# Layernorm of a feed-forward on turned tokens, beside a local attention on one NeuronCore

## The chip, the cores and the metric

The kernel runs on one NeuronCore of a Trainium2 chip. TensorE (PE) multiplies matrices and turns them, VectorE (DVE), ScalarE (ACT) and GpSimd (POOL) work on tiles, and SyncE (SP) issues the DMAs. The metric is the device time of one execution in microseconds. All data is float32.

## The reference, cut to what matters

A decoder layer on `x` of 8 x 256 x 128: a state-space block, a cross-attention, and then six layers of local attention and feed-forward. The change is in the feed-forward of those six layers:

```python
def shift_tokens(t):
    a, s = jnp.split(t, 2, -1)
    s = jnp.pad(s, ((0, 0), (1, 0), (0, 0)))[:, :-1]
    return jnp.concatenate([a, s], -1)

def ffn_layer(x, g, bln, W1, b1, W2, b2):
    mu = x.mean(-1, keepdims=True)
    var = ((x - mu) ** 2).mean(-1, keepdims=True)
    xn = (x - mu) / jnp.sqrt(var + 1e-05) * g + bln
    hg = xn @ W1 + b1
    a, gate = jnp.split(hg, 2, -1)
    return a * jax.nn.gelu(gate, approximate=False) @ W2 + b2

for i in range(DEPTH):
    x = attn_layer(shift_tokens(x), Wqkv[i], q_scale[i], k_scale[i], Wo[i]) + x
    x = ffn_layer(shift_tokens(x), ln_g[i], ln_b[i], W1[i], b1[i], W2[i], b2[i]) + x
```

Mean and variance go over the 128 features of a token.

## The kernel before, in words

Activations lie with the 128 features on the partitions and tokens along the free axis. A pair of batches is one tile of 128 x 512 (`x3[p]`), a batch is 256 columns of it.

Stages one and two (state space, cross-attention) end near 690 us. The third stage runs the list `seq` of 48 entries (six layers times eight batches) through a table written out by hand, `slots` (L1178). `run(n)` (L1212) goes once through its four rows for each batch and calls each named step for batch `n`, `n + 1`, `n + 2` or `n - 1`, so several batches are in flight. The steps that matter here:

- `query_key` (L881): two products into `qk_ps` (L875), two VectorE products with the rotation tables (L892, L893), two GpSimd adds (L896) and ScalarE's squares `sq` (L898). `squares` adds them up (L905), `root` takes the roots on ScalarE (`ss`, `rn`, through `inv_root`, L98), `normalise` multiplies on GpSimd (L924).
- `value` (L916): `v_ps` (L875) and its copy by ScalarE (L918).
- `turn` (L926): eight transposes into `qkT_ps` (L931) and a copy by ScalarE into `qT` (L938) or `kz` (L941).
- `scores` (L979), `masked` (L991), `peak` (L1000, and L1001 on GpSimd), `weigh` (exp of `pw` on ScalarE), `add_weights` (L1012, L1013, and L1014 on GpSimd).
- `turn_weights` (L1016): four transposes into `pT_ps` (L1021), copied by ScalarE (L1025). `attend` (L1038, L1046) and `project_out` (`y_ps`, L1052 and L1060) follow.
- `"ff"`, once a row, and `"late"`, in odd runs, take the next step of `feed_forward` (L1067), a generator that handles one pair during eight rows. There are 23 such pairs; the last pair of the last layer is taken in two halves.

In `feed_forward` before the change, `late` shifts tokens into `xs` (L1087 to L1089). Then, for each half `c` of the pair, TensorE multiplies `xs` with the full 128x128 matrix `mean_w` (all entries 1/128), which gives the mean of each token on every partition (`ln_mu`, L1101). VectorE subtracts (L1102), ScalarE squares (L1103). One product with `mean_w` over all 512 columns gives the variance (`ln_var`, L1106), ScalarE takes Ln and Exp, VectorE multiplies (L1108) and ScalarE adds the bias (L1109). The products of the feed-forward (`f_ps`, L1122) read the result `xn`.

PSUM tiles come from three groups: `big` (two buffers of two banks: `qk_ps`, `v_ps`, `qkT_ps`, `f_ps`), `s` (two buffers of one bank, banks 6 and 7: `ln_mu`, `ln_var`, `pT_ps`, `y_ps`, part of `f_ps`) and `two`. A new tile waits for the readers of the tile whose buffer it takes. TensorE and VectorE execute in the order in which the code calls them (`manual_schedule`, L1360). The order on ScalarE and GpSimd is chosen by the framework's scheduler when the program is built; each engine then works strictly in its order.

Of the kernel before, what the change touches and what calls it, by code (L numbers as in the profile page):

```python
# [9 lines left out]
FP = mybir.dt.float32  # L10
AF = mybir.ActivationFunctionType
ALU = mybir.AluOpType
AX = mybir.AxisListType

P = 128
B, S, D = 8, 256, 128
NPAIR = B // 2
TP = 2 * S
# [31 lines left out]
def decoder_kernel(ctx: ExitStack, tc: tile.TileContext, a: dict, out: bass.AP):  # L50
    nc = tc.nc
    V, A, G, T = nc.vector, nc.scalar, nc.gpsimd, nc.tensor
# [3 lines left out]
    lnp = ctx.enter_context(tc.tile_pool(name="lnp", bufs=2))  # L56
# [5 lines left out]
    def ps_big(name):  # L62
        return banks[-1].tile([P, 1024], FP, tag="big", name=name)

    def ps_s(name):
        return banks[-1].tile([P, 512], FP, tag="s", name=name)
# [10 lines left out]
    ident = keep.tile([P, P], FP, name="ident")  # L77
# [3 lines left out]
    mean_w = keep.tile([P, P], FP, name="mean_w")  # L81
    G.memset(mean_w, 1.0 / D)
    eps_t = keep.tile([P, 1], FP, name="eps_t")
# [5 lines left out]
    def col(name, i=0, n=P):  # L89
        o = _OFF[name] + i  # L90
        return cols[:n, o : o + 1]
# [3 lines left out]
    def with_table(f, *args, **kw):  # L95

        with tc.issue_after(table[-1].ins) if table else ExitStack():
            return f(*args, **kw)  # L98
# [3 lines left out]
    def load_table(name="natural_log_exp_and_others"):  # L102

        late = name == "exp_and_others" and logs
        with tc.issue_after(logs[-1].ins) if late else ExitStack():
            table.append(tc.keep_in_program_order(A.preload_act_table_set(name)))

    def inv_root(dst, src, bias=0.0):

        logs.append(with_table(A.activation, dst, src, AF.Ln, bias=bias))  # L110
        return with_table(A.activation, dst, dst, AF.Exp, scale=-0.5)
# [189 lines left out]
    with (  # L301
# [450 lines left out]
        for p in range(NPAIR):  # L752
            c = pairs[p]
# [313 lines left out]
    def feed_forward(d, p, b=None):  # L1067


        w1, w2 = wts[d][1:3]  # L1070
        at = slice(0, TP) if b is None else slice(b * S, (b + 1) * S)
        m = at.stop - at.start
        x = x3[p][:, at]
        if b == 0:

            t0, t1 = (pools3["w"].tile([P, INNER], FP, tag="wqkv", name="fw", bufs=4) for _ in range(2))
            xs, hh = t0[:, :m], t0[:, m : 4 * m]
            xn, gts = t1[:, :m], [t1[:, (1 + j) * m : (2 + j) * m] for j in range(3)]
        else:
            xs = pools3["b"].tile([P, TP], FP, name="fxs", bufs=1)[:, :m]  # L1080
            xn = pools3["b"].tile([P, TP], FP, name="fxn", bufs=1)[:, :m]
            hh, gts = None, []
        parts = [slice(i, i + S) for i in range(0, m, S)]

        def late(i):

            G.memset(xs[HD:, i : i + 1], 0.0)  # L1087
            A.copy(xs[:HD, i : i + S], x[:HD, i : i + S])
            A.copy(xs[HD:, i + 1 : i + S], x[HD:, i : i + S - 1])  # L1089

        for c in parts:
            late(c.start)
            if len(parts) > 1 and not c.start:
                yield
        if len(parts) == 1:
            yield
        xc = lnp.tile([P, TP], FP, name="ln_xc")[:, :m]
        sq = lnp.tile([P, TP], FP, name="ln_sq")[:, :m]
        for c in parts:
            mu = ps_s("ln_mu")[:, :S]  # L1100
            T.matmul(mu, lhsT=mean_w, rhs=xs[:, c], start=True, stop=True)  # L1101
            V.tensor_tensor(xc[:, c], xs[:, c], mu, ALU.subtract)  # L1102
            A.activation(sq[:, c], xc[:, c], AF.Square)  # L1103
            yield
        var = ps_s("ln_var")[:, :m]
        T.matmul(var, lhsT=mean_w, rhs=sq, start=True, stop=True)  # L1106
        inv_root(sq, var, eps_t)
        V.scalar_tensor_tensor(xn, xc, col("ff_g", d), sq, ALU.mult, ALU.mult)  # L1108
        A.activation(xn, xn, AF.Identity, bias=col("ff_b", d))  # L1109
        yield  # L1110
        if b != 0:
            hh = pools3["b"].tile([P, 3 * TP], FP, name="fh", bufs=1)[:, : 3 * m]
        hh = hh.rearrange("p (j t) -> p j t", j=3)

        def up(i, blocks):

            if blocks[0] < 2:
                pr = ps_big("f_ps")
            for j in blocks:
                f0, n = FB[j]  # L1120
                o = (pr[:, j * TP : j * TP + m] if j < 2 else ps_s("f_ps")[:, :m])[:n]
                T.matmul(  # L1122
                    o, lhsT=w1[:, i * DFF + f0 : i * DFF + f0 + n], rhs=xn, start=True, stop=True
                )
                yield j, n, o

        def product(j, n, o):
            V.scalar_tensor_tensor(
                hh[:n, j, :], o, col("ff_b1", d * 6 + j, n), gts[j][:n], ALU.add, ALU.mult
            )  # L1130

        gates = list(up(1, (0, 1, 2)))
        yield

        for j, n, o in gates:
            if b != 0:
                gts.append(pools3["b"].tile([P, TP], FP, name="fg", bufs=3)[:, :m])
            with tc.issue_after(turned[-1].ins), tc.issue_after(rooted[-1].ins):
                A.activation(gts[j][:n], o, AF.Gelu, bias=col("ff_b1", d * 6 + 3 + j, n))
        load_table()  # L1140
        if b != 0:
            yield
        for blocks in ((2,), (0, 1)):
            for block in list(up(0, blocks)):
                product(*block)
            yield
        for c in parts:
            y_ps = ps_s("f2_ps")[:, :S]
            for j, (f0, n) in enumerate(FB):
                T.matmul(y_ps, lhsT=w2[:n, j, :], rhs=hh[:n, j, c], start=(j == 0), stop=(j == 2))  # L1150
            V.scalar_tensor_tensor(x[:, c], y_ps, col("ff_b2", d), x[:, c], ALU.add, ALU.add)
            yield
# [48 lines left out]
    queue, turned, rooted, copied = [], [], [], []  # L1201
# [10 lines left out]
    def run(n):  # L1212
        nonlocal ff
        for f, *args in slots:
            k, *args = args or [0]
            if f == "ff" or (f == "late" and n % 2):
                next(ff, None)
            elif f == "late":
                pass
            elif f == "end":  # L1220
                if k != n % 2:
                    next(end)
            elif 0 <= n + k < len(seq) and (f, n + k, *args) not in done:
                f(n + k, *args)
                if f is project_out and args[0]:
                    d, b = seq[n + k]
                    last = d == DEPTH - 1
                    if b % 2:
                        ff = feed_forward(d, b // 2)
                        next(ff)  # L1230
                    elif last and b == B - 2:
                        queue.extend((feed_forward(d, b // 2, 0), finish(b // 2, 0)))
                    if last and b % 2 and b > 1:
                        queue.append(finish(b // 2 - 1))
# [27 lines left out]
    with tc.tile_pool(name="s2", bufs=2, reuse_waits="tile") as sp:  # L1262
# [52 lines left out]
        for p in range(NPAIR):  # L1315
# [17 lines left out]
            for hb in range(NHB):  # L1333
                T.matmul(
                    y_ps, lhsT=w2["wo"][:, hb, :], rhs=oT[:, hb, :], start=(hb == 0), stop=(hb == NHB - 1)
# [11 lines left out]
    with ExitStack() as st:  # L1347
# [12 lines left out]
        with tc.manual_schedule(engines={mybir.EngineType.PE, mybir.EngineType.DVE}):  # L1360
            shift(1)
            for n in range(-1, len(seq)):
                run(n)
            project_out(len(seq) - 1, 0)
            attend(len(seq) - 1, 1)
            for _ in ff:
                pass
            next(end)
            project_out(len(seq) - 1, 1)
            tail = feed_forward(DEPTH - 1, NPAIR - 1, 1)  # L1370
            queue.append(finish(NPAIR - 2))
            while queue:
                next(tail, None)
                next(end)
            for _ in tail:
                pass
            for _ in finish(NPAIR - 1, 1):
                pass
# [86 lines left out]
```

## Time and profile before

| what | value |
|---|---|
| median of 3 runs | 2244.76 us (2239.37 to 2244.81) |
| span of the profiled execution | 2235.6 us |
| median above that span | 9.2 us |
| TensorE clock granted, mean | 0.969 |
| TensorE busy | 2096.8 us (94%) |
| VectorE busy | 1743.8 us (78%) |
| GpSimd busy | 1636.2 us (73%) |
| ScalarE busy | 1422.2 us (64%) |

The page does not list a time of the profiled execution apart from its span, so the median stands for what lies around it. A span runs from the first to the last instruction. In the views below a row gives the start, the duration, the engine, the line and the tiles written and read; in brackets is how long the engine sat idle before and who released it. Matmuls on TensorE overlap, so how long it is occupied is read from one start to the next. "PEld" is the weight load of a matmul.

### The profile page before, as it was taken

How to read it: one execution, taken by the hardware profiler on the slowest of the kernel's cores; microseconds unless marked ns; L12 is line 12 of the kernel's file. 1: busy time of each engine (PE TensorE's matmuls, PEld its weight loads, DVE VectorE, ACT ScalarE, POOL GpSimd, SP SyncE). 2: the span in 40 equal slices, each digit the busy share in tenths (PEclk: the TensorE clock that was granted, in tenths of full speed). 3: DMA queues.
4: the chain of work that ended last, by engine and by line, in shares of the span. 5: the costliest groups of instructions: out<-in, count | busy, mean ns of one | idle time of the engine just before them, and what ended most of it. 6: DMA issues, size and time to landing. Idle time of an engine off the chain costs nothing.

```text
span 2235.6 us, 77068 instructions
## 1 busy us (share of the span) xinstructions
PE 2096.8 (94%) x32482; PEld 1314.8 (59%) x32482; DVE 1743.8 (78%) x2533; ACT 1422.2 (64%) x2432; POOL 1636.2 (73%) x1440
## 2 busy tenths in 40 slices
PE   7787879999998999999999999999999999999986
PEld 3232334444445766666767767676767767676663
DVE  5988986353467988888888888888888888888762
ACT  4544546455556776777767677777767677777554
POOL 3988985132268988888888888888888888888750
PEclk8888889999999999999999999999999999999998
DMA  4434431000204444334443434343443434333330
GB/s 124 119 104 100 105 102 31 1 5 1 83 7 68 71 71 95 67 71 75 74 88 71 79 65 94 68 79 67 75 88 69 78 67 84 68 65 64 65 62 10
DMA packets 438326, 155.41 MB, mean 70 GB/s; under 512 B 401886, under 2 KB 418140, under 8 KB 437852
## 3 DMA queue, kind: packets, MB, share of 16 engines
q1 hardware_dynamic: 437500, 150.10, 34.2%
q8 instruction: 255, 4.18, 0.8%
q14 instruction: 91, 0.75, 0.1%
q10 hardware_dynamic: 480, 0.38, 0.1%
HBM read 54.68 MB, written 1.31 MB: 25 GB/s over the span
## 4 chain that ended last, share of the span: by engine, by line
PE 73%; DVE 13%; ACT 7%; issue 4%; POOL 3%; DMA 0%; SPq 0%; DVEq 0%; POOLq 0%; ACTq 0%
PE qk_ps L875 13%; PE y_ps L1052 8%; PE qkT_ps L931 7%; PE o_ps L1038 7%; PE f_ps L1122 6%; PE v_ps L875 6%; PE s_ps L979 5%; DVE m L691 4%; PE pT_ps L1021 3%; PE f_ps L1150 3%; PE o_ps L1296 2%; PE pr L279 2%; PE s_ps L1277 2%; DVE wz L721 2%; ACT ln_sq L98 1%
## 5 line engine op out<-in xcount | busy, mean ns | idle before, releaser
L896 POOL TENSOR_TENSOR qk<-qk,rb 128x512 f32<-128x512 f32 x384 | 481.0, 1275 | 49.0 <-DVE rb L893 30.6
L924 POOL TENSOR_TENSOR qk<-qk,rn 128x1024 f32<-128x1024 f32 x192 | 365.5, 1904 | 12.8 <-ACT rn L98 12.8
L875 PE MATMUL qk_ps<-wqkv,xs 128*128 128x512 f32 x768 | 363.3, 595 | 2.4 <-ACT kz L941 1.4
L1001 POOL TENSOR_TENSOR pw<-pw,mx 128x512 f32<-128x512 f32 x192 | 202.1, 1052 | 164.6 <-DVE mx L1000 164.3
L898 ACT ACTIVATE sq<-qk_ps 128x1024 f32<-128x1024 f32 x192 | 197.0, 1026 | 165.8 <-PE o_ps L1038 122.6
L892 DVE TENSOR_TENSOR qk<-qk_ps,tab 128x1024 f32<-128x1024 f32 x192 | 228.9, 1192 | 66.6 <-PE qk_ps L875 65.1
L905 DVE TENSOR_REDUCE ss<-sq 128x16 f32<-128x1024 f32 x192 | 229.4, 1195 | 6.2 <-ACT sq L898 6.1
L893 DVE TENSOR_TENSOR rb<-qk_ps,tab 128x1024 f32<-128x1024 f32 x192 | 233.3, 1215 | 0.0
L1014 POOL TENSOR_TENSOR pw<-pw,mx 128x512 f32<-128x512 f32 x192 | 200.4, 1044 | 39.1 <-ACT fxn L1109 32.0
L1286 POOL TENSOR_TENSOR ws<-w 128x512 f32<-128x512 f32 x64 | 81.4, 1272 | 196.8 <-ACT w L98 154.1
L1052 PEld LDWEIGHTS y_ps<-oT,wo 128*128 128x128 f32 x1536 | 186.2, 192 | 46.6 <-issue 33.5
L931 PE MATMUL qkT_ps<-ident,qk 128*128 128x128 f32 x1536 | 210.6, 280 | 2.9 <-POOL qk L924 2.9
L1052 PE MATMUL y_ps<-oT,wo 128*128 128x128 f32 x1536 | 187.5, 275 | 1.9 <-ACT pT L1025 1.6
L1046 DVE STREAM_TRANSPOSE oT<-o_ps 128x512 f32<-128x512 f32 x192 | 126.1, 695 | 80.9 <-PE o_ps L1038 80.9
L875 PEld LDWEIGHTS qk_ps<-wqkv,xs 128*128 128x128 f32 x768 | 131.2, 191 | 97.2 <-issue 92.7
L979 PEld LDWEIGHTS s_ps<-kz,qT 64*32 64x32 f32 x12288 | 138.2, 105 | 74.5 <-issue 33.4
L875 PE MATMUL v_ps<-wqkv,xs 128*128 128x512 f32 x384 | 180.5, 592 | 0.3 <-ACT sq L898 0.3
L931 PEld LDWEIGHTS qkT_ps<-ident,qk 128*128 128x128 f32 x1536 | 165.9, 141 | 23.0 <-POOL qk L924 3.8
L98 ACT ACTIVATE ab<-dt,aa 128x512 f32<-128x512 f32 x128 | 87.6, 689 | 143.1 <-DVE m L691 142.9
L726 POOL TENSOR_TENSOR dw<-wz 128x512 f32<-128x512 f32 x128 | 133.9, 1046 | 56.1 <-DVE wz L721 56.1
L691 DVE TENSOR_TENSOR_SCAN m<-dw,ab 128x256 f32<-128x256 f32 x256 | 160.9, 669 | 12.8 <-POOL mc L693 11.4
L1038 PE MATMUL o_ps<-vz,pT 64*32 64x64 f32 x12288 | 168.0, 225 | 1.7 <-issue 1.7
(217 smaller groups left out, 4178.7 us busy)
## 6 DMA issues: line engine op xcount, KB each, us to landing
vz<-v SPq DMA_DIRECT2D x1152, 64.0 KB, 2.2
rows<-bc_dram SPq DMA_DIRECT2D x126, 256.0 KB, 3.9
vz<-v SPq DMA_DIRECT2D x576, 32.0 KB, 2.1
wqkv<-in_L_ffn_Wqkv SPq DMA_DIRECT2D x18, 512.0 KB, 4.4
wo<-in_L_ffn_Wo SPq DMA_DIRECT2D x48, 64.0 KB, 2.6
w<-in_L_ffn_W SPq DMA_DIRECT2D x6, 341.0 KB, 3.1
t_in<-in_x SPq DMA_DIRECT2D x4, 256.0 KB, 3.4
wkv<-in_L_xattn_Wkv SPq DMA_DIRECT2D x1, 1024.0 KB, 7.9
```

Of the source, the lines that this page charges most:

```text
L691: V.tensor_tensor_scan(m[:, t], i["dw"][:, t], i["ab"][:, t], 0.0, ALU.add, ALU.mult)
L875: T.matmul(pr[:, i * 512 : (i + 1) * 512], lhsT=got[n]["xs"][:, tb * P : (tb + 1) * P], rhs=thirds[seq[n][0], c][:, i * 512 : (i + 1) * 51 ...
L892: V.tensor_tensor(t, p3, cs, ALU.mult)
L893: V.tensor_tensor(rb, p3, sn, ALU.mult)
L896: G.tensor_tensor(t[:, :, o], t[:, :, o], rb[:, :, f], ALU.add)
L905: V.tensor_reduce(got[n]["ss"][:, 2 * c + tb, :], got[n]["sq"], AX.X, ALU.add)
L924: G.tensor_tensor(t, t, r, ALU.mult)
L931: T.transpose(t_ps[:, hb * P : (hb + 1) * P], t[:, 2 * hb : 2 * hb + 2, :].rearrange("p h d -> p (h d)"), ident,)
L979: T.matmul(s_ps[i * W : (i + 1) * W, e, c : c + 2 * W], lhsT=qT[r, 4 * g + i, j * W : (j + 1) * W], rhs=kz[r, 4 * g + i, k0 : k0 + 2 * W], ...
L1001: G.tensor_tensor(pw, pw, mx[:, 0].unsqueeze(3).to_broadcast([P, 4, 2, 2 * W]), ALU.subtract)
L1038: T.matmul(o_ps[i * W : (i + 1) * W, e, c : c + HD], lhsT=pT[r, j, i * W : (i + 1) * W], rhs=vz[r, j, i, :], start=True, stop=True, tile_p ...
L1052: T.matmul(y_ps[:, :P], lhsT=wts[d][0][:, hb, :], rhs=got[n]["oT", wh][:, hb // 4, (hb // 2) % 2, :].rearrange("p (w h q) -> p h w q", w=4 ...
```

## The change

The layernorm of the feed-forward is done with tokens on the partitions. For each half, TensorE turns two blocks of 128 tokens into PSUM (`ft_ps`); VectorE takes mean and variance of each token with `bn_stats` and `bn_aggr` and negates the mean; ScalarE takes the root of the variance (a column of numbers now, not a full tile); GpSimd multiplies the negated mean with it; ScalarE normalises each block out of PSUM with these as scale and bias. One step later TensorE turns the two blocks back (`fn_ps`), and ScalarE applies gain and bias on the way out of PSUM. Both shifts are issued in the first step instead of one in the first and one in the second; the number of steps is the same.

```diff
         for c in parts:
             late(c.start)
-            if len(parts) > 1 and not c.start:
-                yield
-        if len(parts) == 1:
-            yield
-        xc = lnp.tile([P, TP], FP, name="ln_xc")[:, :m]
-        sq = lnp.tile([P, TP], FP, name="ln_sq")[:, :m]
-        for c in parts:
-            mu = ps_s("ln_mu")[:, :S]
-            T.matmul(mu, lhsT=mean_w, rhs=xs[:, c], start=True, stop=True)
-            V.tensor_tensor(xc[:, c], xs[:, c], mu, ALU.subtract)
-            A.activation(sq[:, c], xc[:, c], AF.Square)
-            yield
-        var = ps_s("ln_var")[:, :m]
-        T.matmul(var, lhsT=mean_w, rhs=sq, start=True, stop=True)
-        inv_root(sq, var, eps_t)
-        V.scalar_tensor_tensor(xn, xc, col("ff_g", d), sq, ALU.mult, ALU.mult)
-        A.activation(xn, xn, AF.Identity, bias=col("ff_b", d))
+        yield
+        xt = lnp.tile([P, TP], FP, name="ln_xc")[:, :m]
+        rs = lnp.tile([P, 4], FP, name="ln_rs")
+        st = lnp.tile([P, 4, 6], FP, name="bn_st")
+        mv = lnp.tile([P, 4, 2], FP, name="bn_mv")
+
+        def blocks_of(c):
+            return range(c.start // P, c.stop // P)
+
+        def tokens(c):
+
+            tp = ps_s("ft_ps")
+            js = blocks_of(c)
+            for i, j in enumerate(js):
+                T.transpose(tp[:, i * P : (i + 1) * P], xs[:, j * P : (j + 1) * P], ident)
+            for i, j in enumerate(js):
+                V.bn_stats(st[:, j, :], tp[:, i * P : (i + 1) * P])
+                V.bn_aggr(mv[:, j, :], st[:, j, :])
+            jj = slice(js[0], js[-1] + 1)
+            V.tensor_scalar(mv[:, jj, 0], mv[:, jj, 0], -1.0, None, ALU.mult)
+            rooted.append(inv_root(rs[:, jj], mv[:, jj, 1], eps_t))
+            G.tensor_tensor(mv[:, jj, 0], mv[:, jj, 0], rs[:, jj], ALU.mult)
+            for i, j in enumerate(js):
+                A.activation(
+                    xt[:, j * P : (j + 1) * P], tp[:, i * P : (i + 1) * P], AF.Identity,
+                    bias=mv[:, j, 0:1], scale=rs[:, j : j + 1],
+                )
+
+        def turned_back(c):
+            tp = ps_s("fn_ps")
+            for i, j in enumerate(blocks_of(c)):
+                T.transpose(tp[:, i * P : (i + 1) * P], xt[:, j * P : (j + 1) * P], ident)
+            A.activation(
+                xn[:, c], tp[:, :S], AF.Identity, bias=col("ff_b", d), scale=col("ff_g", d)
+            )
+
+        for i, c in enumerate(parts):
+            if i:
+                turned_back(parts[i - 1])
+            tokens(c)
+            yield
+        turned_back(parts[-1])
         yield
```

## The prediction

> **What bounds the kernel now.** I read the page's busy shares and slices first, then the busy time by stage, then the waits of the feed-forward's lines, then the timeline of one pair.
>
> ```profile
> PE 2096.8 (94%) x32482; PEld 1314.8 (59%) x32482; DVE 1743.8 (78%) x2533; ACT 1422.2 (64%) x2432; POOL 1636.2 (73%) x1440
> ...
> PE   7787879999998999999999999999999999999986
> ...
> PEclk8888889999999999999999999999999999999998
> ```
>
> TensorE is at 9 tenths in every slice of the local-attention stage. The table by stage (columns: stretch, its length, busy time of each engine, granted clock) says how full that is:
>
> ```profile
> 720.00:2160.00 1440.00, 1419.43 (x29044) 999.55 (x29032) 1228.33 (x1739) 1019.96 (x1776) 1185.11 (x1027) 1.00 0.41 74
> ```
>
> 1419 of 1440 us at full clock, VectorE 85%, GpSimd 82%, ScalarE 71%. The first `f_ps` product of each pair starts at 790.34 and, twenty pairs later, at 2047.41 in the chain that ended last: 62.85 us a pair. So what TensorE gains or loses in a pair, the kernel gains or loses. Its one regular wait is this one (us, times, longest, over 15 pairs):
>
> ```profile
> PE f_ps L1122 <- ACT sq L898: 9.4, 15, 0.8
> ```
>
> That is 0.63 us a pair. Now the stretch in which the old mean products stand; the changed steps take the same places.
>
> ```profile
> 1145.50 1.09 PE L931 MATMUL qkT_ps<-ident,qk 128*128 128x128 f32 x8
> ...
> 1146.43 0.60 PE L1101 MATMUL ln_mu<-fxs,mean_w 128*128 128x256 f32 x2
> ...
> 1146.87 0.60 PE L1021 MATMUL pT_ps<-ident,pw 128*128 128x128 f32 x4
> ...
> 1147.30 1.88 PE L875 MATMUL qk_ps<-wqkv,xs 128*128 128x512 f32 x4
> ...
> 1148.00 0.67 DVE L1000 TENSOR_REDUCE mx<-pw 128x8 f32<-128x512 f32 x1
> ...
> 1148.75 1.04 POOL L1001 TENSOR_TENSOR pw<-pw,mx 128x512 f32<-128x512 f32 x1 [1.55 <-DVE mx L1000]
> ...
> 1149.76 1.90 POOL L924 TENSOR_TENSOR qk<-qk,rn 128x1024 f32<-128x1024 f32 x1
> 1149.83 0.63 ACT L98 ACTIVATE pw<-pw 128x512 f32<-128x512 f32 x1 [0.38 <-POOL pw L1001]
> ...
> 1150.94 1.01 ACT L918 COPY v<-v_ps 128x1024 f32<-128x1024 f32 x1 [0.48 <-PE v_ps L875]
> ...
> 1152.09 1.03 ACT L898 ACTIVATE sq<-qk_ps 128x1024 f32<-128x1024 f32 x1
> 1152.33 0.86 PEld L931 LDWEIGHTS qkT_ps<-ident,qk 128*128 128x128 f32 x8
> ...
> 1153.46 1.01 ACT L938 COPY qT<-qkT_ps 128x1024 f32<-128x1024 f32 x1 [0.34 <-PE qkT_ps L931]
> ...
> 1153.69 0.60 PE L1021 MATMUL pT_ps<-ident,pw 128*128 128x128 f32 x4
> ```
>
> Read starts, not durations, on TensorE: four transposes occupy it from 1146.87 to 1147.30. And see that `v` is copied out at 1150.94 to 1151.95 and the `qkT_ps` transposes, which take over that PSUM buffer, start at 1152.33: 0.38 us of room.
>
> **The change, part by part** (per pair of batches).
>
> *TensorE's work.* Removed: `ln_mu` twice, 0.44 and 0.43 us by starts (1146.43 to 1146.87), and `ln_var`, 0.86 (1160.36 to 1161.22): 1.73. Added: eight transposes at 0.108 (0.43/4): 0.86. Alone that is -0.87 us a pair: -0.22 where `ft_ps` replaces the first mean, nothing where `fn_ps` and `ft_ps` replace the second, -0.64 where the last `fn_ps` replaces `ln_var`.
>
> The trace has a mean of 280 ns for one L931 transpose, but that is pipelined latency; the starts say 108. [...] The starts decide.
>
> *VectorE.* Removed 2 x 0.41 (L1102) and 1.13 (L1108), with a 0.52 wait on `ln_sq`; added four bn_stats (0.269, row of `bn_st`), four aggregates (0.174) and two negations (as the 128x8 reciprocal, 0.203): 2.18 against 1.95. In the first two rows VectorE gets 1.09 in place of 0.41; its waits there (0.53 for `s_ps`) cover most, and nothing on TensorE's path waits. Should bn_stats out of PSUM cost half as much again, the chain below still has 0.6 in hand.
>
> *ScalarE.* Removed 2 x 0.42, 0.69, 0.65, 0.71; added four roots of 128x2 (0.289 + 0.205 each pair of them), four normalises of 128x128 and two evictions of 128x256. The sum is about +1 us on an engine with 18 us free: nothing by itself. The order is what counts. In the program as built, 21 of the 23 full pairs have on ScalarE: exp of `pw`, the two roots of `ln_rs`, two normalises, **then** the copy of `v`, `sq`, copy of `qT`, eviction of `fn_ps`, and only later the copy of `pT`. On GpSimd the small product stands between L924 and L1014.
>
> *Stall A, new.* The normalises wait for that product, and it waits behind L924. L924 ends at 1151.66. The roots are ready by then: L1000 ends 1148.67, statistics 1.09, ScalarE free of `pw` at 1150.46, roots 0.5: 1151.0. The product: between 0.09 (a memset, L865) and 0.46 (128x128, L815); 128x64 takes 0.32, so I take 0.2. ScalarE starts 0.04 later (as 1149.79 to 1149.83): 1151.90. A normalise: 0.48 by the 128x128 row with the same operands but SBUF source (L541); the other end is a plain copy, 0.585 at 512 and 1.011 at 1024 elements, so 0.83 ns an element and 0.27 at 128. I take 0.48, the nearer form: 1152.88. The copy of `v`, queued behind: 1153.92. TensorE restarts 0.06 after such a copy (sq to `f_ps`): 1153.98 for 1152.33. **+1.65**, bounds +1.1 and +1.9. L1014 moves by 0.25, and its reader `pT` comes later.
>
> [...]
>
> *Stall B, new.* `fn_ps` of the first part, `ft_ps` of the second and `pT_ps` follow each other in two PSUM banks, and as built `pT_ps` gets the bank of `fn_ps`. So it waits for the eviction, which is queued behind the copy of `qT`. From the start of the `qkT` transposes: 1.13 to the copy (1152.33 to 1153.46), 1.01 for it, the eviction 0.56 (128x512 with bias and scale 0.771, L259, less 256 x 0.83 ns; other end 0.37, a Ln of 128x256), 0.08 of hops: 2.78, where today `pT` follows after 1.36. **+1.42**, low end +1.2. Where the product of part two is late, `y_ps` is not: the second `ft_ps` has the other bank.
>
> *Row after.* -0.64 for `ln_var`. And the 0.63 wait before `f_ps` ends: VectorE no longer has L1108 with its wait (1.67) ahead of L893, so `sq` ends near 1170.2, just when TensorE arrives: **-0.6**, bounds 0 and -0.7.
>
> *Other.* Both shifted copies are now issued in one step; as built they stand in the same places of ScalarE's order, so nothing. No DMA is added or moved.
>
> *Sum.* 1.65 + 1.42 - 0.64 - 0.6 = +1.83 us a pair, times 21: +38.4. The last two full pairs and the two halves run where TensorE waits anyway (2160 to 2235: 50 of 75 us busy) with chains of about equal length: nothing, within 3 us. The span goes from 2235.6 to 2274. The median run, 2244.76, lies 9.2 above the span; this is kept: **2283 us**. The ends of the terms give +1.0 and +2.7 a pair: 2266 and 2302.
>
> **The rivals.**
>
> 1. *TensorE only gets its 0.87 us, and faster.* For it: TensorE is 99% busy in the stage, and every other engine has room. If `v` were copied in time, 21 x (0.87 + 0 to 0.6) = 18 to 31 us go: 2214 to 2226. It decides if the normalises end before about 1151.2, that is if they don't wait for L924. Against: the order as built and L924's 1.90. Chance 0.10.
> 2. *One stall only.* A without B, or B without A, leaves +0.2 to +0.4 a pair: 2248 to 2254, nearly no change. For it: B is 1.4 us of queueing whose pieces each have rows, but the order in the first moments after A may differ. Chance 0.10.
> 3. *More than two stalls.* The roots of `ss` or the copy of `pT`, now behind the eviction, also make `y_ps` late (it has 0.9 in hand by the same sums), or the wait before `f_ps` grows: one more microsecond and up, 2302 to 2325. Chance 0.10.
>
> That the change does something else than said is excluded by the built program: 96 normalises, 192 transposes.
>
> **How the numbers follow.** Forecast 0.70, at 2283, own range 2266 to 2302. Leaving out rival 1 and the upper part of rival 3 gives 2245 to 2312. A change under 0.3%, about what can be told apart here, means 2238 to 2251.5: 0.07, from rival 2's lower part. Faster 0.10, slower 0.83.
>
> **What would show it.** In the profile after: a regular TensorE wait before L931 put down to ScalarE's copy of `v`, 1 to 2 us, and one before `pT_ps` put down to the `fn_ps` eviction, 1.2 to 1.5, each some 21 times; no wait of `f_ps` on `sq`; the pair's period at 64.7; TensorE's busy share lower by 2 to 4 points. The prediction is wrong if the copy of `v` starts within 0.3 us of its product's end, or if a normalise takes under 0.3.

## The result, and the profile after

The changed kernel takes 2259.78 us (median of 4 runs, 2256.48 to 2265.77), the kernel before 2242.15 us (median of 4, 2239.37 to 2244.81): a ratio of 1.0086, interval 1.0064 to 1.0107 (the quotient of the two medians is 1.0079). It is slower by 17.6 us. The forecast was slower by 38 us (2283). The direction held, but the change is less than half of what was forecast. The time lies below the forecast's own range of 2266 to 2302, and inside the wider one of 2245 to 2312.

The profiled execution of the changed kernel took 2256.48 us, the shortest of its four, and its span is 2254.7, so 1.8 us lie around a span. First the page: busy time and share of each engine, TensorE's busy tenths and its clock, and the group of the `qkT_ps` transposes (busy, mean ns | idle before, what ended it).

```profile
PE 2071.9 (92%) x32528; PEld 1307.4 (58%) x32528; DVE 1756.5 (78%) x2700; ACT 1432.5 (64%) x2545; POOL 1646.4 (73%) x1488
...
PE   7787889999998999999999999999999999999986
...
PEclk8888889999999999999999999999999999999999
...
L931 PE MATMUL qkT_ps<-ident,qk 128*128 128x128 f32 x1536 | 210.0, 280 | 33.3 <-ACT v L918 29.9
```

TensorE has 25 us less to do and is done 19 us later. The tenths hide it, since 96% is a 9 as much as 99% is. The busy time by stage, over the same stretch as before, shows it:

```profile
720.00:2160.00 1440.00, 1377.48 (x28447) 977.07 (x28435) 1223.18 (x1862) 1021.20 (x1862) 1178.80 (x1058) 1.00 0.40 73
```

TensorE was busy for 1419 of 1440 us and is busy for 1377 now, at the same clock of 1.00; VectorE, ScalarE and GpSimd hardly moved. The idle time must have an owner, and the waits from 1100 to 2060 us (15 pairs; us in total, times, longest) name two on TensorE and one behind them on ScalarE:

```profile
ACT ln_xc L1116 <- POOL bn_mv L1114: 33.0, 30, 1.2
...
PE qkT_ps L931 <- ACT v L918: 21.1, 15, 1.5
...
PE pT_ps L1021 <- ACT fxn L1125: 18.4, 15, 1.2
```

These are stalls A (1.41 us on average) and B (1.23), once a pair each. The old wait of `f_ps` on `sq` is gone. The timeline of one pair shows how they come about:

```profile
1151.44 1.09 PE L931 MATMUL qkT_ps<-ident,qk 128*128 128x128 f32 x8
...
1155.74 1.90 POOL L924 TENSOR_TENSOR qk<-qk,rn 128x1024 f32<-128x1024 f32 x1
...
1156.66 0.20 ACT L98 ACTIVATE ln_rs<-ln_rs 128x2 f32<-128x2 f32 x1
...
1157.61 0.20 POOL L1114 TENSOR_TENSOR bn_mv<-bn_mv,ln_rs 128x2 f32<-128x2 f32 x1
...
1157.84 0.81 ACT L1116 ACTIVATE ln_xc<-ft_ps,bn_mv,ln_rs 128x128 f32<-128x128 f32 x2 [0.96 <-POOL bn_mv L1114]
...
1158.54 1.01 ACT L918 COPY v<-v_ps 128x1024 f32<-128x1024 f32 x1
...
1159.60 1.09 PE L931 MATMUL qkT_ps<-ident,qk 128*128 128x128 f32 x8 [1.28 <-ACT v L918]
...
1160.73 1.01 ACT L938 COPY qT<-qkT_ps 128x1024 f32<-128x1024 f32 x1 [0.26 <-PE qkT_ps L931]
...
1161.64 0.57 ACT L1125 ACTIVATE fxn<-fn_ps,cols 128x256 f32<-128x256 f32 x1
...
1162.35 0.63 PE L1021 MATMUL pT_ps<-ident,pw 128*128 128x128 f32 x4 [1.22 <-ACT fxn L1125]
```

Read it as a relay: L924 ends, the small product takes 0.20, two normalises follow, then the copy of `v` that was queued behind them, then TensorE. And again: transposes, copy of `qT`, eviction of `fn_ps`, and only then `pT_ps`. ScalarE was idle for 0.96 us before the normalises while the copy of `v` stood behind them in its queue.

**Where the time went.** The table compares TensorE's starts, the same step in both kernels. Its next to last row ends with the first `f_ps` product, which waited before the change and does not after it:

```profile
1168.52 2.84 PE L1122 MATMUL f_ps<-fxn,w 128*128 128x512 f32 x6 [0.57 <-ACT sq L898]
```

```profile
1175.53 2.84 PE L1147 MATMUL f_ps<-fxn,w 128*128 128x512 f32 x6
```

| from start to start | before | after | difference |
|---|---|---|---|
| `qkT` (row before) to `qkT` | 6.83 | 8.16 | +1.33 (A) |
| `qkT` to `pT` | 1.36 | 2.75 | +1.39 (B) |
| `pT` to `qkT` | 5.74 | 5.67 | -0.07 |
| `qkT` to `pT` (was `ln_var`) | 1.79 | 1.15 | -0.64 |
| `pT` to `qkT` | 5.63 | 5.44 | -0.19 |
| `qkT` to `f_ps` | 1.67 | 0.92 | -0.75 |
| sum for this pair | | | +1.07 |

Over twenty pairs the first `f_ps` product of a pair, in the chain that ended last, goes from 790.69 to 2071.58 in the changed kernel: 64.04 us a pair for 62.85, **+1.19**. The difference of the two spans, 19.1 us, is then: 0.35 up to the first of these starts, 23.8 in the twenty pairs, 2.9 in the last two full pairs (127.48 for 124.61), and **-7.9 at the end**, from the last full pair's first `f_ps` to the end of the span (55.64 for 63.58). In the timeline these products of the changed kernel start 0.16 to 0.17 us earlier than in the chain; the period is the same by both, and the end is then -7.8. The prediction set the last pairs and the end at nothing.

At the end two halves of a pair are in flight, and ScalarE has Gelus (L1139, L1164) and roots (L98) to do, and from the one to the other the trace of this stretch has a table load of 1.28 us. This is ScalarE before, in that stretch:

```profile
2199.09 0.47 ACT L1139 ACTIVATE fw<-f_ps,cols 128x256 f32<-128x256 f32 x1 [0.37 <-PE f_ps L1122]
2199.59 1.28 ACT L98 ACT_TABLE_LOAD   x1
2200.88 0.47 ACT L98 ACTIVATE ln_sq<-ln_var,eps_t 128x256 f32<-128x256 f32 x1
2201.37 1.28 ACT L1139 ACT_TABLE_LOAD   x1
2202.67 0.47 ACT L1139 ACTIVATE fw<-f_ps,cols 128x256 f32<-128x256 f32 x1
2203.16 1.28 ACT L98 ACT_TABLE_LOAD   x1
2204.45 0.42 ACT L98 ACTIVATE ln_sq<-ln_sq 128x256 f32<-128x256 f32 x1
2204.89 1.28 ACT L1139 ACT_TABLE_LOAD   x1
```

and after:

```profile
2223.76 0.20 ACT L98 ACTIVATE ln_rs<-ln_rs 128x2 f32<-128x2 f32 x1
2223.99 1.28 ACT L1164 ACT_TABLE_LOAD   x1
2225.28 0.47 ACT L1164 ACTIVATE fw<-f_ps,cols 128x256 f32<-128x256 f32 x1
```

Before, the roots of one half stand between the Gelus of the other, and each turn pays a load of 1.28 us; after, the roots are through before the first Gelu. The place to look is one word of the diff: the roots are now put on the list `rooted`, behind which the Gelus are issued. Experiments e1 and e2 test it.

### The profile page after: what moved, and what is told of

It reads as the page before. It is cut to its first block, busy times and chain, and to the rows that moved or that the text cites. A ratio compares the mean times of both kernels' runs of the same rounds, so it can differ in the third digit from the quotient of the medians.

```text
span 2254.7 us, 77482 instructions
## 1 busy us (share of the span) xinstructions
PE 2071.9 (92%) x32528; PEld 1307.4 (58%) x32528; DVE 1756.5 (78%) x2700; ACT 1432.5 (64%) x2545; POOL 1646.4 (73%) x1488
## 4 chain that ended last, share of the span: by engine, by line
PE 73%; DVE 11%; ACT 6%; issue 5%; POOL 3%; DMA 1%; SPq 1%; ACTq 0%; DVEq 0%; POOLq 0%
PE qk_ps L875 13%; PE qkT_ps L931 8%; PE y_ps L1052 8%; PE o_ps L1038 7%; PE v_ps L875 6%; PE f_ps L1147 5%; PE s_ps L979 5%; DVE m L691 4%; PE pT_ps L1021 4%; PE f_ps L1175 3%; PE o_ps L1321 2%; PE pr L279 2%; PE s_ps L1302 2%; DVE wz L721 2%; PE y_ps L1359 1%
## 5 line engine op out<-in xcount | busy, mean ns | idle before, releaser
L924 POOL TENSOR_TENSOR qk<-qk,rn 128x1024 f32<-128x1024 f32 x192 | 365.8, 1905 | 18.5 <-ACT rn L98 18.5
L1001 POOL TENSOR_TENSOR pw<-pw,mx 128x512 f32<-128x512 f32 x192 | 202.3, 1054 | 198.5 <-DVE mx L1000 197.5
L98 ACT ACTIVATE ab<-dt,aa 128x512 f32<-128x512 f32 x128 | 87.6, 688 | 143.3 <-DVE m L691 143.1
L693 POOL TENSOR_TENSOR mc<-m,rows 128x512 f32<-128x512 f32 x128 | 167.8, 1312 | 3.5 <-DVE m L691 1.4
```

The lines of the kernel that those rows point to most:

```text
L924: G.tensor_tensor(t, t, r, ALU.mult)
L1001: G.tensor_tensor(pw, pw, mx[:, 0].unsqueeze(3).to_broadcast([P, 4, 2, 2 * W]), ALU.subtract)
```

## The experiments

**Theory.** A and B cost what TensorE waits; the rest is the freed `ln_var` and `sq` waits and, at the end, the list of roots. **Rivals.** That VectorE's statistics cost the time; that the end comes from the shorter chain of the new layernorm and not from the list; that A and B hide one another. Each ratio compares a kernel with the kernel before on the same chip, whose median was 2238.4 to 2242.2 from one set of runs to the next; the ratios differ from the quotients of the medians by up to 0.0012. The period is that of the first `f_ps` over twenty pairs, "end" is from the last full pair's first `f_ps` to the end of the span, both in the chain; they come from one execution of each kernel.

| kernel | median, us | ratio, interval | span | period | end |
|---|---|---|---|---|---|
| before | 2242.15 | 1 | 2235.6 | 62.85 | 63.6 |
| after | 2259.78 | 1.0086 (1.0064 to 1.0107) | 2254.7 | 64.04 | 55.6 |
| roots off the list (e1) | 2265.80 | 1.0110 (1.0097 to 1.0124) | 2265.4 | 64.10 | 61.0 |
| before, roots on the list (e2) | 2234.64 | 0.9973 (0.9963 to 0.9983) | 2234.4 | 62.83 | 63.2 |
| turned back at once (e3) | 2221.75 | 0.9916 (0.9902 to 0.9929) | 2221.0 | 62.61 | 55.8 |
| `v` first (e4) | 2241.45 | 1.0006 (0.9996 to 1.0017) | 2239.1 | 63.05 | 57.7 |
| both (e5) | 2207.26 | 0.9857 (0.9842 to 0.9872) | 2206.1 | 61.76 | 55.5 |
| statistics twice (e6) | 2314.40 | 1.0327 (1.0307 to 1.0347) | 2314.8 | 66.74 | 57.5 |
| product on ScalarE (e8) | 2248.15 | 1.0040 (1.0027 to 1.0053) | 2241.9 | 63.42 | 54.6 |
| e6, negation on ScalarE (e9) | 2282.85 | 1.0177 (1.0158 to 1.0195) | 2281.9 | 64.93 | 61.3 |
| after, negation on ScalarE (e10) | 2260.60 | 1.0081 (1.0061 to 1.0100) | 2259.0 | 64.02 | 58.6 |

### The end: e1 and e2

e1 is the changed kernel with the roots off the list, e2 the kernel before with its roots on it.

```diff
-            rooted.append(inv_root(rs[:, jj], mv[:, jj, 1], eps_t))
+            inv_root(rs[:, jj], mv[:, jj, 1], eps_t)
```

```diff
-        inv_root(sq, var, eps_t)
+        rooted.append(inv_root(sq, var, eps_t))
```

> The changed kernel, but the roots of the layernorm are not put on the list of roots behind which the Gelus are issued. Theory: that list is why the last two halves end 7.9 us earlier after the change (63.6 us from the last full pair's f_ps to the end before, 55.6 after), since the Gelus of one half no longer alternate with the roots of the other. Then that stretch goes back to about 63 us, the period of a pair stays at 64.0, and the span is near 2262. Rival: the new chain of a half is simply shorter; the stretch stays at 55.6 and the span at 2255.

> The kernel before, with one word of the change: the roots of its layernorm are put on the list behind which the Gelus are issued. Theory: the period of a pair stays at 62.85 and only the end gets shorter, by 5 to 8 us: span 2228 to 2231, ratio about 0.997. Rival (the gain at the end is that of the short chain on tokens): no change, 2235.6.

Off the list, the end grows from 55.6 to 61.0 us (about 63 was expected) at nearly the same period (64.10 for 64.04), and the median by 6.0, though single runs of the two kernels overlap (up to 2265.77 and from 2261.15). On the list, the kernel before gains 5.1 us (2234.64 for 2239.74 in the same set of runs; the interval of the ratio, 0.9963 to 0.9983, is clear of 1). The groups of table loads, by the line that pays for them (how many | busy us, mean ns | idle before), show where it comes from, 66 in the kernel before and 62 in e2. Kernel before:

```profile
L106 ACT ACT_TABLE_LOAD x37 | 47.5, 1283 | 2.4 <-issue 1.8
...
L1139 ACT ACT_TABLE_LOAD x27 | 34.6, 1283 | 0.5
...
L98 ACT ACT_TABLE_LOAD x2 | 2.6, 1283 | 0.0
```

and e2, beside the same 37 of L106:

```profile
L1139 ACT ACT_TABLE_LOAD x25 | 32.1, 1283 | 0.4
```

So the list is worth about 5 us in the kernel before, and four loads of 1.283 us are 5.1. With the new layernorm the list saves two loads only: the changed kernel has 62 and e1 has 64, again with 37 of L106:

```profile
L1164 ACT ACT_TABLE_LOAD x26 | 33.4, 1283 | 0.4
...
L98 ACT ACT_TABLE_LOAD x1 | 1.3, 1283 | 0.0
```

That is 2.6 of the 5.4 us by which e1's end is longer; the rest of it is not settled. Nor is the part of the 7.9 that e1 doesn't give back, some 2 us. In the profiled executions the granted clock at the end was 0.83 before, 0.92 after and 0.85 in e1, and it varied between 0.80 and 0.93 among the kernels of this study. In e2's profiled run it was 0.80 there, which may be why its end (63.2) and its span (2234.4, for 2228 to 2231 expected) do not show the gain that its median does.

### Stall B: e3

Both halves are turned back in one step, after the second half's normalises, and leave PSUM in one eviction. Nothing is left between the copy of `qT` and the transposes of `pw`.

```diff
+            n = c.stop - c.start
...
-                xn[:, c], tp[:, :S], AF.Identity, bias=col("ff_b", d), scale=col("ff_g", d)
+                xn[:, c], tp[:, :n], AF.Identity, bias=col("ff_b", d), scale=col("ff_g", d)
...
-        for i, c in enumerate(parts):
-            if i:
-                turned_back(parts[i - 1])
+        for c in parts:
             tokens(c)
             yield
-        turned_back(parts[-1])
+        turned_back(slice(0, m))
```

> The changed kernel, with both halves turned back in one step (four transposes into one fn_ps, one eviction of 128x512) in the place of the second. Theory of two stalls: the wait of pT_ps for the eviction of fn_ps goes (1.39 us a pair), 0.2 us of transposes move into the next row, the wait for the copy of v stays: period from 64.04 to about 62.85, span about 2230, ratio 0.997. Rival (the cost lies in the many small instructions on VectorE and ScalarE, not in what waits for what): period and span stay at 64.0 and 2255.

The period falls by 1.43 us to 62.61, where B had cost 1.39 by starts (62.85 was expected). In the waits of the same stretch one of the two is left, nearly as large as it was:

```profile
PE qkT_ps L931 <- ACT v L918: 20.0, 15, 1.5
```

The price of B is confirmed, and the late eviction has no price of its own. With A still in it this kernel already beats the kernel before.

### Stall A: e4 and e8

e4 issues the first half's normalises behind the copy of `v`, and changes no operation. e8 keeps the order and takes the product off GpSimd: two operations of ScalarE on one number a partition, which wait for nothing behind L924.

```diff
-        A.copy(t, proj(n, 2, tb, "v_ps"))
+        with_v = A.copy(t, proj(n, 2, tb, "v_ps"))
...
+        while behind_v:
+            with tc.issue_after(with_v.ins):
+                behind_v.pop()()
...
+            def scaled():
+                for i, j in enumerate(js):
+                    A.activation(
+                        xt[:, j * P : (j + 1) * P], tp[:, i * P : (i + 1) * P], AF.Identity,
+                        bias=mv[:, j, 0:1], scale=rs[:, j : j + 1],
+                    )
+
+            if len(parts) > 1 and not c.start:
+                behind_v.append(scaled)
+            else:
+                scaled()
```

```diff
-            G.tensor_tensor(mv[:, jj, 0], mv[:, jj, 0], rs[:, jj], ALU.mult)
+            for j in js:
+                A.activation(
+                    mv[:, j, 0:1], mv[:, j, 0:1], AF.Identity, scale=rs[:, j : j + 1],
+                )
```

> The changed kernel, with the two normalises of the first half issued behind the copy of v instead of before it. Theory of two stalls: the wait of the qkT_ps transposes for the copy of v goes (1.33 us a pair), that of pT_ps stays: period from 64.04 to about 62.7, span about 2227, ratio 0.996. Rival (cost of the small instructions themselves): nothing changes, 2255.

> The changed kernel, with the product of negated mean and root done by two small ScalarE instructions instead of one on GpSimd, so that nothing waits behind L924. Theory of two stalls: the normalises start about 0.45 us earlier, stall A shrinks by that, B stays: period 63.6, span about 2246. Rival (ScalarE's added work is what the pair pays): four more instructions of some 0.25 us, 1 us a pair more, span about 2275.

In e4 the wait behind `v` is gone, yet the period falls by 0.99 only, to 63.05, less than the 1.33 of A and less than expected (62.7). Its waits in the same stretch say where the rest is:

```profile
PE pT_ps L1024 <- ACT fxn L1136: 24.2, 14, 1.8
```

and so does the timeline of one pair:

```profile
1150.61 1.01 ACT L918 COPY v<-v_ps 128x1024 f32<-128x1024 f32 x1
...
1151.52 0.81 ACT L1120 ACTIVATE ln_xc<-ft_ps,bn_mv,ln_rs 128x128 f32<-128x128 f32 x2
...
1151.72 1.09 PE L934 MATMUL qkT_ps<-ident,qk 128*128 128x128 f32 x8
...
1152.52 1.02 ACT L898 ACTIVATE sq<-qk_ps 128x1024 f32<-128x1024 f32 x1 [0.19 <-DVE rb L893]
...
1153.44 1.01 ACT L941 COPY qT<-qkT_ps 128x1024 f32<-128x1024 f32 x1
...
1154.33 0.58 ACT L1136 ACTIVATE fxn<-fn_ps,cols 128x256 f32<-128x256 f32 x1
...
1155.06 0.63 PE L1024 MATMUL pT_ps<-ident,pw 128*128 128x128 f32 x4 [1.81 <-ACT fxn L1136]
```

TensorE turns `qk` sooner, but ScalarE is not free sooner, since the two normalises now stand between the copy of `v` and that of `qT`: the copy of `qT` now starts 1.72 us after the transposes (1151.72 to 1153.44) where in the changed kernel it took 1.13. B grew from 1.23 to 1.73 us a time. So part of the second stall had been hidden in the first.

e8 behaves as the theory says: the wait behind `v` shrinks to 12.3 us in 15 times (0.82) and the period falls by 0.62 to 63.42 (63.6 was expected), while TensorE still waits 18.3 us in 15 times before `pT_ps`. So some 0.6 us of A was GpSimd's queue (L924 and the product), and the rest the normalises themselves in front of `v`.

### Both: e5

e3 and e4 together.

> The changed kernel with both repairs: first half normalised behind the copy of v, both halves turned back in one step. Theory of two stalls: what is left is TensorE's 0.87 us less and the wait of f_ps on sq gone (0.63 to 0.75): period about 61.4, span about 2200, ratio 0.983 to 0.986, faster than both. Rival (the small instructions cost by themselves): at or above the kernel before, 2235 to 2255.

The period falls to 61.76, by 2.28 of the 2.72 that A and B measure. Expected was 61.4; the 0.36 between has no owner in these waits, of which no regular one of TensorE is left:

```profile
PE o_ps L1041 <- issue: 1.5, 4, 0.5
PE qk_ps L875 <- ACT sq L898: 0.7, 4, 0.2
```

At 2207.26 us this kernel beats both: the idea of the change, less work for TensorE, is good for 1.4% (some 0.2 of it the list's, by e2), and the two places of its ScalarE operations turned that into a loss.

### VectorE's statistics: e6, e9 and e10

e6 takes every statistic twice, with the same result. e9 is e6 with the negation of the mean made by ScalarE, e10 the changed kernel with that edit alone.

```diff
-                V.bn_stats(st[:, j, :], tp[:, i * P : (i + 1) * P])
-                V.bn_aggr(mv[:, j, :], st[:, j, :])
+                for _ in range(2):
+                    V.bn_stats(st[:, j, :], tp[:, i * P : (i + 1) * P])
+                    V.bn_aggr(mv[:, j, :], st[:, j, :])
```

```diff
-            V.tensor_scalar(mv[:, jj, 0], mv[:, jj, 0], -1.0, None, ALU.mult)
+            A.activation(mv[:, jj, 0], mv[:, jj, 0], AF.Identity, scale=-1.0)
```

> The changed kernel, with every bn_stats and bn_aggr done twice (the second writes the same numbers again), 0.92 us more on VectorE for a half. Theory of two stalls: the roots were ready 0.75 us before GpSimd came to the product, so the copy of v moves by only 0.2 us: 0.2 to 0.5 us a pair, span 2259 to 2265. Rival (VectorE's added work is what the pair pays): 1.8 us a pair, span about 2293.

> The run with doubled statistics, with one more edit: the negation of the mean (two numbers a partition) is made by ScalarE in place of VectorE. In the run with doubled statistics VectorE's negation took 1.05 us in the median and up to 1.53, and ended when GpSimd's product with rn (L924) ended. Theory: what cost 2.7 us a pair there is that VectorE stood in the negation for as long as GpSimd worked on L924, with TensorE waiting behind it for longer than 2 us and at a lower granted clock after it. Then the period falls from 66.7 to 64.3 to 65.3 us, the mean granted clock from 720 to 1200 us is back at 0.99 or more, and the span is 2262 to 2285 us. Rival: the doubled VectorE work itself (48 x 0.75 us) is what costs; then the period stays at 66.2 to 66.9 and the span at 2300 to 2316.

> The changed kernel with the negation of the mean on ScalarE in place of VectorE. In the changed kernel itself the negation took 0.29 us in the median, at most 0.38, beside GpSimd's work. Theory: there it lies on no path, so the period stays within 0.4 us of 64.04, since ScalarE gets two more small operations of about 0.2 us a pair while it stands idle for a part of stall A; the span is 2249 to 2263 us. Rival: VectorE's negation is a hidden part of the two stalls in the changed kernel too; then the period falls by 0.5 us or more and the span to 2244 or less.

e6 missed all expectations: 2.7 us a pair (0.2 to 0.5 by the theory), for 1.8 us more of VectorE's work. Its timeline shows two things that were not in the theory:

```profile
1176.89 1.91 POOL L924 TENSOR_TENSOR qk<-qk,rn 128x1024 f32<-128x1024 f32 x1
...
1177.76 1.05 DVE L1113 TENSOR_SCALAR bn_mv<-bn_mv 128x2 f32<-128x2 f32 x1
...
1184.43 1.09 PE L1021 MATMUL pT_ps<-ident,pw 128*128 128x128 f32 x4 [2.07 <-ACT fxn L1126]
...
1185.31 3.07 PE L875 MATMUL qk_ps<-wqkv,xs 128*128 128x512 f32 x4
...
1186.33 1.90 POOL L924 TENSOR_TENSOR qk<-qk,rn 128x1024 f32<-128x1024 f32 x1 [0.37 <-ACT rn L98]
...
1186.73 1.53 DVE L1113 TENSOR_SCALAR bn_mv<-bn_mv 128x2 f32<-128x2 f32 x1
```

First, a negation of two numbers a partition takes 1.05 and 1.53 us, and both times it ends when GpSimd's L924 ends (1178.8 and 1188.2). The line's group has the shortest, median and longest ns of the 48 negations. In the changed kernel:

```profile
L1112 DVE TENSOR_SCALAR bn_mv<-bn_mv x48: 168/294/380, 770.4 to 2223.4; 128x2 f32<-128x2 f32 x48
```

and in e6:

```profile
L1113 DVE TENSOR_SCALAR bn_mv<-bn_mv x48: 169/1053/1532, 772.6 to 2283.5; 128x2 f32<-128x2 f32 x48
```

In the changed kernel the same thing happens with the GpSimd operation ahead of L924:

```profile
1154.74 1.04 POOL L1001 TENSOR_TENSOR pw<-pw,mx 128x512 f32<-128x512 f32 x1 [1.46 <-DVE mx L1000]
...
1155.51 0.29 DVE L1112 TENSOR_SCALAR bn_mv<-bn_mv 128x2 f32<-128x2 f32 x1
```

Of its 48 negations 44 start inside L1001 and end 0.02 to 0.04 us after it; they start so late in it that this takes 0.29 to 0.38 us. The four that start while GpSimd is idle take 0.17. In e6 the doubled statistics push 42 of 48 into L924. Second, after a wait of 2.07 us TensorE is slow: four transposes and the product behind them take 0.88 and 3.07 us where the changed kernel has 0.47 and 1.88 after its 1.22. In the stretch from 1184.4 to 1188.0 the granted clock was 0.54. In e6's schedule the first half's normalises also went behind the copy of `v` (1178.08 and 1180.95), as in e4, so e6 and e4 are the pair to compare and not e6 and the changed kernel.

e9 confirms the first point: with the negation on ScalarE, which takes 0.20, the period falls by 1.81 to 64.93, as expected. The clock is where that expectation failed in part: 0.98 from 720 to 1200 us in place of 0.99 or more. Its wait before `pT_ps`, from 1100 to 2060 us:

```profile
PE pT_ps L1021 <- ACT fxn L1126: 29.1, 15, 1.9
```

and the busy times and the clock (third number from the end) in a stretch behind one such wait:

```profile
1169.00:1172.00 3.00, 2.94 (x7) 1.92 (x8) 2.76 (x11) 2.22 (x8) 2.32 (x5) 0.50 0.40 67
```

A wait of 1.94 us ended at 1169.06, and for 3 us the clock granted was a half. It was not so after every such wait: e9 has 21 of 1.93 to 1.95 us between 760 and 2110 us, and in the 3 us behind them the clock was 0.50 to 0.73 in 15 cases and 1.00 in six. So the doubled statistics do cost in this order of ScalarE; by an estimate from these numbers, a clock of 0.98 over 65 us, the clock makes 1.3 us of the 1.88 between e9 and e4, and the rest is not taken apart. In the changed kernel the runs show no price of either: the clock is 1.00 in the stage and e10's period is that of the changed kernel (64.02 for 64.04). That the statistics themselves cost nothing there rests on its timeline, where the roots behind them are ready at 1156.86, 0.75 us before the product starts (1157.61); no run doubles them in that order.

## Why the prediction was wrong, and what it had right

The mechanism held, and terms of the sum failed. The prediction put the change at +38.4 us; between the two spans it is 19.1. In its own terms the steps that failed are stall A, in which a normalise was taken at 0.48 us and measured 0.35 from start to start; the later rows, set at nothing, which gave back 0.26 a pair; and "the last two full pairs and the two halves … nothing", which came to -5.1. Neither of its two signs of a wrong mechanism showed: the copy of `v` starts 1.9 us after its product ends, and a normalise takes 0.45.

- **The bound and the two stalls: right.** A and B stand where the prediction put them, with the releasers that it named and once a pair, and e3, e4 and e5 show that taking them away gives the time back. The `f_ps` wait on `sq` is gone, and TensorE's share fell by 2 points, as said.
- **Stall A, +1.65: measured +1.33.** The step that failed is the normalise at 0.48 us. A pair of them occupies ScalarE for 0.70 (1157.84 to 1158.54), so 0.35 each, for 0.96 by the sum; the product at 0.20 was right to the hundredth. The row that was taken (L541, from SBUF) gives the duration of one operation, which is 0.45 here, while two in a row overlap.
- **Stall B, +1.42: measured +1.39.** Right, by e3 too (-1.43 without it). Its eviction took 0.57 for 0.56.
- **The row after, -0.64: measured -0.64.** Two transposes cost TensorE 0.22 us by starts (1168.95 to 1169.17), as taken from the starts before.
- **The wait before `f_ps`, -0.6: measured -0.75,** a little beyond its bound.
- **Missing:** -0.26 in the two intervals from `pT` to `qkT` of the later rows, which the prediction set at nothing; why they got shorter is not shown. The sum is +1.19 a pair for +1.83: by the terms of the one pair shown, 0.32 from A, 0.03 from B, 0.15 from the wait and 0.26 from these; this pair lies 0.12 below the mean. Up to the last two full pairs it is 14.2 us of the miss (38.4 forecast, 24.2 measured).
- **"The last two full pairs and the two halves … nothing, within 3 us": wrong.** It came to -5.1 in the profiled execution (+2.9 and -7.9). The prediction compared lengths of chains and passed over `rooted.append` in the diff, whose effect is on Gelus of the other half. e1 and e2 show that the list matters; how much of the 7.9 is the list and how much the clock of that execution stays open.
- **9.2 us around the span: wrong.** The profiled run has 1.8; the rest of the 9.2 was the difference between one execution of before and another. That accounts for 7.4 us. Together: 14.2 + 5.1 + 7.4 make the 26.7 between 2283 and the profiled run's 2256.5. The median lies 3.3 above that run.
- **The rivals.** One stall only (2248 to 2254) is what e4 and e3 build; they gave 2241 and 2222. By period they are +0.20 and -0.24 a pair, for +0.2 to +0.4 by the rival, and both have an end 6 to 8 us shorter, which the rival did not count. TensorE only gaining (2214 to 2226) is e5: 2207, with the list in it, which that rival did not count either.

## What to carry to other kernels

When an operation is placed on an engine that has room, ask what is queued behind it there and when its own input comes: here two operations of 0.35 us on an engine with 36% idle time cost 1.3 us a pair of batches, because they waited for GpSimd at the head of a queue that TensorE's buffers hang on. Price such a relay from start to start, and test it by moving one link at a time, since here the second stall in the same queue grew when the first was taken away (1.23 to 1.73 us, e4), and both repairs together gave 2.28 us a pair (e5). Read every line of a diff for order, not only for work: one `append` moved 5 us (e2).

## What the hardware showed that was not expected

- VectorE's negation of 128x2, 0.17 us while GpSimd was idle, ended with the GpSimd product inside which it started: up to 1.53 us with the 1.90 us L924 (e6), and 0.29 to 0.38 with the last third of the 1.04 us L1001 (the changed kernel). Both kernels show it, for two numbers a partition, and e9 shows that moving the negation takes the delay away (0.20 us on ScalarE); why VectorE's operation lasts that long is not shown.
- The granted clock fell to 0.50 to 0.54 for about 3 us after single waits of 1.94 us (e9) and 2.07 us (e6), and stayed at 1.00 after waits of 1.81 us (e4) and 1.5 us (the changed kernel). The length of the wait does not decide alone: of e9's 21 waits of 1.93 to 1.95 us, six left the clock at 1.00. What else counts is not shown.
